# A cross-attention block on one core: reordering the steady loop (query product 7, feature scaling, row loads, query seed)

## The chip, the cores and the metric

The kernel runs on one core of a Trainium2 chip. It is written in a language in which each engine has its own queue and works through it in the order in which the program issues to it; semaphores hold an instruction until what it reads or overwrites is ready. The engines are PE (matrix products; PEld is its loading of weights), DVE (VectorE), ACT (ScalarE), POOL (GpSimd) and SP (SyncE, which here issues nearly all DMAs). The metric is the device time of one execution in microseconds (us), as the median of several runs; lower is better.

## The reference

16 batches of 1024 rows of 512 features attend to 64 context rows each. Rows and context are normalised, scaled and shifted by factors that come from a condition vector; the attention has 16 heads of width 32.

```
xq  = (1 + scale_q[b])  * layernorm(x)       + shift_q[b]
xkv = (1 + scale_kv[b]) * layernorm(context) + shift_kv[b]
q = xq @ Wq + bq;   k, v = split(xkv @ Wkv + bkv)
attn = softmax(q k^T / sqrt(32))             # per batch and head
out = x + (attn v) @ Wp + bp
```

All of it is float32.

## The kernel before

The 16384 rows are worked in 32 blocks of 512 rows (two blocks a batch). Block numbers are `i`; a loop runs over `i = 3 .. 29`, and what comes ahead of it and behind it is written out as straight code. The order of the work is written by hand: no scheduler moves anything, so what stands first in the code stands first in its engine's queue. An iteration works on several blocks at once, in a software pipeline:

- **Block i + 5** is loaded from memory (`load_x`, L119, 1 MB in one DMA). A load for block i + 5 goes into the buffer of block i + 3, of which there are two in turn, and so comes behind `turn(i + 3)`.
- **Block i + 4** has its row statistics taken (`q_stats`, DVE, L294 and L295, two instructions for each of four groups of rows) and their scale computed (`q_scale`, ACT and POOL, L303 to L312).
- **Block i + 3** is normalised (`hidden`, ACT, L335), turned by DVE in 32 x 32 pieces (`turn`, L365, four instructions, into the one buffer `ht`) and moved by 16 DMAs of 64 KB to where rows and features have changed places (`move`, L387, from `ht` to `xt`).
- **Block f = i + 2** has its features scaled and shifted on ACT (`scale_features`, L447, four instructions, in place on `xt`) and sums of its halves formed on POOL (`feature_sums`, L498).
- **Block n = i + 1** has its queries computed. The 512 x 512 matrix product is done in seven half-size products (a Strassen-like scheme): `query_product(n, 1..7)` on PE (L539), eight rows in the trace for each. They go into two PSUM banks. Product 1 starts bank 0; `query_seed` (ACT, L551) copies it into bank 1, where product 2 adds to it; product 7 starts bank 1 anew and product 4 adds to that. In between the finished parts are taken out, by ACT with the bias (`query_out`, L578, two instructions) or by DVE as an addition (`query_added`, L585). So product 4 may not begin before `query_out(n, 7)` has read bank 1, and product 3 not before `query_added(n, 5)` has read bank 0.
- **Block i** has its scores computed (`scores`: PE L670, maxima on DVE L687, copies on ACT L696), the maxima spread (L716) and subtracted on POOL (`subtract`, L729), and the exponentials taken on ACT (`weights(i, 0)` and `weights(i, 1)`, L740). POOL adds the two halves (`total`, L790); DVE sums them (`row_total`, L795) and inverts them, and `inverse_rows` sends the sums through DRAM by one DMA (L813) and four (L815). `swapped` (L745, two DMAs) moves parts of one half into places of the other.
- **Block a = i - 1** has those parts written again by two more exponentials (`again`, ACT, L751), is multiplied with the values (`mix`, PE L860), divided by the row sums (`divided`, DVE L839), and begins its output projection, seven products again: `product(a, 1)`, `product(a, 2)`, `product(a, 7)` (PE L1000), additions to the residual `added` (DVE, L1024), `biased` (ACT, L963: the bias put into a bank that products then add to) and `row_sums` (POOL, L975 to L980). `biased(a, 3)` reuses the bank that `added(a, 2)` reads.
- **Block b = i - 2** ends its projection (products 6, 5, 4, 3) and is stored (L1026).

On SP all DMAs stand in one queue, and a DMA whose data isn't ready holds up those behind it. The program gives them eight semaphores in turn, so each also waits for the eighth DMA ahead of it to land. In an iteration the order on SP is: output stores of b, residual load (L126), rows load (L119), the two swaps (L745), the small store and the four small loads of the row sums (L813, L815), and the 16 moves (L387).

Of the kernel before, what the change touches and what calls it, by code (L numbers as in the profile page):

```python
# [10 lines left out]
AF = mybir.ActivationFunctionType  # L11
# [9 lines left out]
def cross_attention_block(  # L21
# [18 lines left out]
    nc = tc.nc  # L40
# [10 lines left out]
    NB = B * BPB  # L51
# [320 lines left out]
    def features_tile(i):  # L372
        if i in GROUPS:
            pool, tag = (big, "big0") if i == "A" else (qpool, "vb")
            t = pool.tile([P, NC, TB], F32, tag=tag, name=f"xk_{i}", bufs=1)
        else:
            t = qpool.tile([P, 4, NC, NT * 32], F32, tag="xt", name=f"xt_{i}")
        xt_tiles[i] = t
        return t

    def move(i, two=False):

        ht = ht_tiles.pop(i)
        xt = features_tile(i)
        for k in range(4):
            for g in range(4):
                (nc.gpsimd if two and g % 2 else nc.sync).dma_start(  # L387
                    xt[32 * k : 32 * k + 32, g],
                    ht[32 * g : 32 * g + 32, k].rearrange("p c t b -> p c (t b)"),
                )  # L390
# [165 lines left out]
    def query_product(i, n):  # L556
        seven(i, "q", n, (0, 1))

    def query_seed(i):
        seed(i, "q", (0, 1))  # L560
# [183 lines left out]
            at = 64 * g  # L744
            nc.sync.dma_start(s_tiles[i, 1][at : at + 32], s_tiles[i, 0][at + 32 : at + 64])  # L745

    def again(i):
        s = raw_tiles.pop(i)
        for g in range(2):
            at = 64 * g  # L750
            nc.scalar.activation(  # L751
                s_tiles[i, 0][at + 32 : at + 64], s[at : at + 32], AF.Exp, scale=SCALE
            )

    def sums(i, z):
        if z == 0:
# [252 lines left out]
    def added(i, n):  # L1009

        m, o = {1: (0, 0), 2: (0, 0), 6: (0, 1), 7: (1, 1), 5: (1, 1), 4: (0, 1), 3: (1, 0)}[n]
        r = r_tiles[i][:, 2 * m : 2 * m + 2, o * HO : (o + 1) * HO]
        k = acc_bank(i, n)
        a = acc[k].rearrange("p (t h) -> p t h", t=2)
        if i == NB - 1:

            for ts in ((0,), (1,)) if n == 3 else ((0, 1),):
                ts = slice(ts[0], ts[-1] + 1)
                nc.vector.tensor_add(r[:, ts, :], a[:, ts, :], r[:, ts, :])
                if n in (2, 3, 4, 5):  # L1020
                    dst = rows_of(out, i)[:, 2 * m : 2 * m + 2, o * HO : (o + 1) * HO]
                    nc.sync.dma_start(dst[:, ts, :], r[:, ts, :])
            return
        nc.vector.tensor_add(r, a, r)  # L1024
        if n in (3, 4):
            nc.sync.dma_start(  # L1026
                rows_of(out, i)[:, 2 * m : 2 * m + 2, :], r_tiles[i][:, 2 * m : 2 * m + 2, :]
            )
# [421 lines left out]
    for i in range(3, NB - 2):  # L1450
        a, b, n, f = i - 1, i - 2, i + 1, i + 2

        scores(i, 0, crossed=True)
        again(a)
        product(b, 6)
        added(b, 6)
        query_product(n, 1)
        query_seed(n)
        added(b, 7)
        scores(i, 1)  # L1460
        product(b, 5)
        added(b, 5)
        maxima(i)
        subtract(i)
        product(b, 4)
        if i < NB - 3:
            hidden(i + 3, (0, 1, 2))
        query_product(n, 2)
        query_out(n, 2)
        product(b, 3)  # L1470
        spread_rows(a)
        if i < NB - 3:
            hidden(i + 3, (3,))
        added(b, 4)
        added(b, 3)
        biased(a, 2)
        load_residual(i)
        mix(a)
        divided(a)
        row_sums(a, 0)  # L1480
        query_product(n, 6)
        weights(i, 0)
        query_out(n, 6)
        scale_features(f, (0, 1))
        product(a, 1)
        if i + 4 < NB:
            q_stats(i + 4, (0,))
        added(a, 1)
        product(a, 2)
        if i + 4 < NB:  # L1490
            q_stats(i + 4, (1,))
        added(a, 2)
        weights(i, 1)
        total(i)
        query_product(n, 7)
        query_out(n, 7)
        biased(a, 3)
        scale_features(f, (2, 3))
        row_sums(a, 1)
        if i < NB - 3:  # L1500
            turn(i + 3, range(NT))
        if i < NB - 5:
            load_x(i + 5)
        elif i == NB - 3:
            load_residual(NB - 1)
        swapped(i)
        query_product(n, 5)
        query_added(n, 5)
        if i + 4 < NB:
            q_stats(i + 4, (2,))  # L1510
        query_product(n, 4)
        query_added(n, 4)
        if i + 4 < NB:
            q_stats(i + 4, (3,))
        query_product(n, 3)
        query_out(n, 3)
        feature_sums(f)
        product(a, 7)
        row_total(i)
        inverse_rows(i)  # L1520
        if i + 3 < NB:
            move(i + 3)
        if i + 4 < NB:
            q_scale(i + 4)

    y, z = NB - 2, NB - 1
    residual(y - 1)
    scores(y, 0, crossed=True)
    again(y - 1)
    product(y - 2, 6)  # L1530
    added(y - 2, 6)
    query_product(z, 1)
    query_seed(z)
    added(y - 2, 7)
    scores(y, 1)
    product(y - 2, 5)
# [125 lines left out]
```

## Time and profile before

| | |
|---|---|
| median of 3 runs | 1034.76 us (1033.57 to 1035.35) |
| the profiled execution | 1033.38 us, span 1031.6 us |
| granted PE clock, mean over the span | 0.996 |
| PE, DVE, POOL, ACT busy | 97%, 84%, 78%, 72% of the span |
| ahead of the loop's scores(3, 0) | 162.85 us |
| the loop, 27 iterations | 791.56 us (162.85 to 954.41) |
| behind it | 77.19 us (954.41 to 1031.60) |

The span runs from the first to the last instruction of the profiled execution. The timelines list instructions in the order of time: start, length, engine, line, operation, what it writes and reads, shape and count (neighbours of one kind are merged), and in brackets how long the engine stood idle before it and what ended that. Lengths of matmuls overlap, since they are pipelined; how fast PE goes is read from start to start. A wait for several things is put down to the one that the profile saw last, which need not be the true one.

### The profile page before, as it was taken

How to read it: one execution, taken by the hardware profiler on the slowest of the kernel's cores; microseconds unless marked ns; L12 is line 12 of the kernel's file. 1: busy time of each engine (PE TensorE's matmuls, PEld its weight loads, DVE VectorE, ACT ScalarE, POOL GpSimd, SP SyncE). 2: the span in 40 equal slices, each digit the busy share in tenths (PEclk: the TensorE clock that was granted, in tenths of full speed). 3: DMA queues.
4: the chain of work that ended last, by engine and by line, in shares of the span. 5: the costliest groups of instructions: out<-in, count | busy, mean ns of one | idle time of the engine just before them, and what ended most of it. 6: DMA issues, size and time to landing. Idle time of an engine off the chain costs nothing.

```text
span 1031.6 us, 19531 instructions
## 1 busy us (share of the span) xinstructions
PE 1004.2 (97%) x7181; PEld 754.1 (73%) x7181; DVE 862.1 (84%) x1174; ACT 743.0 (72%) x1081; POOL 806.6 (78%) x518
## 2 busy tenths in 40 slices
PE   8999898899999999999999999999999999999998
PEld 7877556677777777777777777777777777777646
DVE  6777668789898888898898988898998988876695
ACT  3777567677887778777887787777877787777630
POOL 4566687788888788988788888988887888888861
PEclk9999999999999999999999999999999999999999
DMA  9574645555455555565455555565455555445222
GB/s 313 166 198 124 151 120 146 174 179 185 135 142 175 150 174 177 174 183 176 135 152 174 150 173 179 172 185 166 143 148 160 165 174 173 139 145 158 72 86 85
DMA packets 114880, 164.41 MB, mean 159 GB/s; under 512 B 35000, under 2 KB 46288, under 8 KB 112992
## 3 DMA queue, kind: packets, MB, share of 16 engines
q1 hardware_dynamic: 114400, 162.62, 52.5%
q8 instruction: 57, 0.93, 0.4%
q0 software_dynamic: 384, 0.54, 0.3%
q14 instruction: 39, 0.32, 0.1%
HBM read 79.21 MB, written 34.60 MB: 110 GB/s over the span
## 4 chain that ended last, share of the span: by engine, by line
PE 62%; SPq 10%; DMA 7%; POOL 6%; DVE 6%; ACT 5%; issue 4%; DVEq 0%; ACTq 0%; POOLq 0%
PE pq L539 25%; PE pp L1000 24%; SPq L387 8%; PE ps L670 5%; PE po L860 3%; POOL s L729 3%; POOL sum L790 2%; DMA xt<-ht 2%; DMA ltd<-lt 2%; ACT xt L447 1%; ACT p L740 1%; PE pp L898 1%; PE pk_A L539 1%; PE pv_A L539 1%; DVE lt L795 1%
## 5 line engine op out<-in xcount | busy, mean ns | idle before, releaser
L729 POOL TENSOR_TENSOR s<-s,mb 128x2048 f32<-128x2048 f32 x64 | 290.6, 4564 | 128.0 <-DVE mb L716 126.2
L687 DVE TRANSPOSE_TENSOR_REDUCE m<-ps 128x32 f32<-128x1024 f32 x128 | 151.1, 1217 | 31.2 <-PE ps L670 31.1
L696 ACT COPY s<-ps 128x1024 f32<-128x1024 f32 x128 | 126.6, 1014 | 62.5 <-PE ps L670 39.0
L1000 PE MATMUL pp<-w_p_sb,ot 128*128 128x256 f32 x720 | 165.7, 380 | 1.0 <-DVE ot L839 0.4
L578 ACT ACTIVATE qt<-pq,bias_t 128x256 f32<-128x256 f32 x256 | 105.4, 462 | 67.3 <-PE pq L539 67.3
L1024 DVE TENSOR_TENSOR r<-pp,r 128x512 f32<-128x512 f32 x203 | 131.8, 670 | 25.3 <-PE pp L1000 19.1
L1000 PEld LDWEIGHTS pp<-w_p_sb,ot 128*128 128x128 f32 x720 | 136.7, 190 | 20.8 <-issue 1.4
L790 POOL TENSOR_TENSOR sum<-s,p 128x2048 f32<-128x2048 f32 x28 | 127.0, 4535 | 4.6 <-ACT p L740 3.8
L1000 PEld LDWEIGHTS pp<-WT,s 128*128 128x128 f32 x480 | 86.6, 190 | 56.9 <-issue 17.6
L539 PE MATMUL pq<-xt_sums,w_q_sums 128*128 128x256 f32 x512 | 123.4, 385 | 0.0
L539 PE MATMUL pq<-xt,w_q_sums 128*128 128x256 f32 x512 | 121.6, 381 | 1.7 <-DVE qt L585 1.7
L539 PE MATMUL pq<-xt,w_q_sb 128*128 128x256 f32 x512 | 121.9, 381 | 1.4 <-ACT pq L551 0.8
L539 PEld LDWEIGHTS pq<-xt_sums,w_q_sums 128*128 128x128 f32 x512 | 95.1, 190 | 36.3 <-issue 24.8
L1000 PE MATMUL pp<-WT,s 128*128 128x256 f32 x480 | 119.4, 392 | 0.2 <-POOL s L979 0.2
L1000 PE MATMUL pp<-WT,ot 128*128 128x256 f32 x480 | 113.6, 380 | 0.5 <-POOL ot L976 0.5
L751 ACT ACTIVATE s<-s 32x2048 f32<-32x2048 f32 x56 | 106.9, 1908 | 5.7 <-DMA p<-s 4.3
L539 PEld LDWEIGHTS pq<-xt,w_q_sb 128*128 128x128 f32 x512 | 96.7, 190 | 17.9 <-ACT pq L551 2.5
L539 PEld LDWEIGHTS pq<-xt,w_q_sums 128*128 128x128 f32 x512 | 97.9, 191 | 15.4 <-DVE qt L585 2.1
L447 ACT ACTIVATE xt<-xt,ss_q 128x512 f32<-128x512 f32 x124 | 94.0, 808 | 16.3 <-DMA xt<-ht 12.2
L1000 PEld LDWEIGHTS pp<-WT,ot 128*128 128x128 f32 x480 | 91.2, 190 | 13.9 <-POOL ot L976 0.9
L335 ACT ACTIVATE x<-x,rstdq 128x512 f32<-128x512 f32 x128 | 97.0, 805 | 5.1 <-POOL rstdq L312 4.4
L498 POOL TENSOR_TENSOR xt_sums<-xt 128x512 f32<-128x512 f32 x64 | 81.5, 1274 | 14.6 <-ACT xt L447 7.8
(187 smaller groups left out, 1632.8 us busy)
## 6 DMA issues: line engine op xcount, KB each, us to landing
x<-in_x_dram SPq DMA_DIRECT2D x32, 1024.0 KB, 7.6
r<-in_x_dram SPq DMA_DIRECT2D x32, 1024.0 KB, 5.5
xt<-ht SPq DMA_DIRECT2D x488, 64.0 KB, 2.0
out_dram<-r SPq DMA_DIRECT2D x58, 512.0 KB, 3.7
p<-s SPq DMA_DIRECT2D x56, 256.0 KB, 4.7
out_dram<-r SPq DMA_DIRECT2D x11, 256.0 KB, 2.2
wss_kv<-in_L_xcond_Wss_kv_dram SPq DMA_DIRECT2D x4, 512.0 KB, 8.0
wss_q<-in_L_xcond_Wss_q_dram SPq DMA_DIRECT2D x4, 512.0 KB, 10.7
```

The costliest lines, as they stand in the source:

```text
L335: nc.scalar.activation(dst, src, AF.Identity, bias=rstd[:, 1, j : j + 1], scale=rstd[:, 0, j : j + 1])
L387: (nc.gpsimd if two and g % 2 else nc.sync).dma_start(xt[32 * k : 32 * k + 32, g], ht[32 * g : 32 * g + 32, k].rearrange("p c t b -> p c ( ...
L447: nc.scalar.activation(xt[:, :, c, :], xt[:, :, c, :], AF.Identity, scale=ss["q"][:, c, b : b + 1], bias=ss["q"][:, NC + c, b : b + 1],)
L539: nc.tensor.matmul(out_, lhsT=lhsT, rhs=rhs, start=new and m == 0 and c == 0, stop=c == HC - 1, skip_group_check=True,)
L578: nc.scalar.activation(dst, src, AF.Identity, bias=bq_t[:, o : o + 1])
L687: nc.vector.tensor_reduce(m_tiles[i][:, z, 2 * e : 2 * e + 2, :], s_banks[i, z][e].rearrange("p r (j a) -> p r j a", a=32), AX.X, ALU.max, ...
L696: nc.scalar.copy(s_tiles[i, z][:, 2 * e : 2 * e + 2, :], s_banks[i, z][e])
L729: eng.tensor_tensor(s_tiles[i, z], s_tiles[i, z], mb_tiles[i], ALU.subtract)
L751: nc.scalar.activation(s_tiles[i, 0][at + 32 : at + 64], s[at : at + 32], AF.Exp, scale=SCALE)
L790: nc.gpsimd.tensor_tensor(t, s_tiles[i, 0], s_tiles[i, 1], ALU.add)
L1000: nc.tensor.matmul(acc[k][:, t * HO : (t + 1) * HO], lhsT=rows[:, c, t * P : (t + 1) * P], rhs=cols[:, c, :], start=n == 2 and t == 0 and ...
L1024: nc.vector.tensor_add(r, a, r)
```

## The change

Four things change place in the loop; no instruction's work changes.

- `query_product(n, 7)` and `query_out(n, 7)` stand ahead of `product(a, 2)` and of `weights(i, 1)`, not behind them.
- `scale_features(f)` is done in one piece, behind `biased(a, 3)`, not two instructions ahead of `weights(i, 1)` and two behind `biased(a, 3)`. `turn(i + 3)` stands ahead of `added(a, 2)`.
- `load_x(i + 5)` leaves its place ahead of `swapped(i)` and goes between the fourth and the fifth of the 16 moves, at the iteration's end.
- `query_seed(n)` stands between the two exponentials of `again`, not behind both. This is also done in block y = 30, behind the loop.

```diff
@@ -378,11 +378,14 @@
         xt_tiles[i] = t
         return t
 
-    def move(i, two=False):
-
-        ht = ht_tiles.pop(i)
-        xt = features_tile(i)
-        for k in range(4):
+    def move(i, two=False, ks=range(4)):
+
+        if ks[0] == 0:
+            features_tile(i)
+        ht, xt = ht_tiles[i], xt_tiles[i]
+        if ks[-1] == 3:
+            ht_tiles.pop(i)
+        for k in ks:
             for g in range(4):
                 (nc.gpsimd if two and g % 2 else nc.sync).dma_start(
                     xt[32 * k : 32 * k + 32, g],
@@ -744,13 +747,13 @@
             at = 64 * g
             nc.sync.dma_start(s_tiles[i, 1][at : at + 32], s_tiles[i, 0][at + 32 : at + 64])
 
-    def again(i):
-        s = raw_tiles.pop(i)
-        for g in range(2):
-            at = 64 * g
-            nc.scalar.activation(
-                s_tiles[i, 0][at + 32 : at + 64], s[at : at + 32], AF.Exp, scale=SCALE
-            )
+    def again(i, g):
+        at = 64 * g
+        nc.scalar.activation(
+            s_tiles[i, 0][at + 32 : at + 64], raw_tiles[i][at : at + 32], AF.Exp, scale=SCALE
+        )
+        if g == 1:
+            raw_tiles.pop(i)
 
     def sums(i, z):
         if z == 0:
@@ -1451,11 +1454,12 @@
         a, b, n, f = i - 1, i - 2, i + 1, i + 2
 
         scores(i, 0, crossed=True)
-        again(a)
+        again(a, 0)
         product(b, 6)
         added(b, 6)
         query_product(n, 1)
         query_seed(n)
+        again(a, 1)
         added(b, 7)
         scores(i, 1)
         product(b, 5)
@@ -1481,27 +1485,24 @@
         query_product(n, 6)
         weights(i, 0)
         query_out(n, 6)
-        scale_features(f, (0, 1))
         product(a, 1)
         if i + 4 < NB:
             q_stats(i + 4, (0,))
         added(a, 1)
-        product(a, 2)
+        query_product(n, 7)
+        query_out(n, 7)
         if i + 4 < NB:
             q_stats(i + 4, (1,))
-        added(a, 2)
         weights(i, 1)
         total(i)
-        query_product(n, 7)
-        query_out(n, 7)
-        biased(a, 3)
-        scale_features(f, (2, 3))
-        row_sums(a, 1)
+        product(a, 2)
         if i < NB - 3:
             turn(i + 3, range(NT))
-        if i < NB - 5:
-            load_x(i + 5)
-        elif i == NB - 3:
+        added(a, 2)
+        biased(a, 3)
+        scale_features(f)
+        row_sums(a, 1)
+        if i == NB - 3:
             load_residual(NB - 1)
         swapped(i)
         query_product(n, 5)
@@ -1519,18 +1520,22 @@
         row_total(i)
         inverse_rows(i)
         if i + 3 < NB:
-            move(i + 3)
+            move(i + 3, ks=(0,))
+            if i < NB - 5:
+                load_x(i + 5)
+            move(i + 3, ks=(1, 2, 3))
         if i + 4 < NB:
             q_scale(i + 4)
 
     y, z = NB - 2, NB - 1
     residual(y - 1)
     scores(y, 0, crossed=True)
-    again(y - 1)
+    again(y - 1, 0)
     product(y - 2, 6)
     added(y - 2, 6)
     query_product(z, 1)
     query_seed(z)
+    again(y - 1, 1)
     added(y - 2, 7)
     scores(y, 1)
     product(y - 2, 5)
```

The order on ACT, from the first exponential of block i = 14 to copy 3 of its neighbour's queries, is before (`s` and `p` are the scores and weights, `qt` the queries, `pq` the banks of their products by number, `xt` the features; "x2" counts neighbours of one kind):

```order
L740 ACTIVATE s_0_4333<-s_0_4333 128x2048
L578 ACTIVATE qt_4398<-pq_1_4345,bias_t 128x2x4x32 x2
L447 ACTIVATE xt_4286<-xt_4286,ss_q 128x4x128 x2
L740 ACTIVATE p_4467<-s_1_4371 128x2048
L578 ACTIVATE qt_4398<-pq_7_4471,bias_t 128x2x4x32 x2
L963 COPY pp_3_4478<-b_diff 128x512
L447 ACTIVATE xt_4286<-xt_4286,ss_q 128x4x128 x2
L578 ACTIVATE qt_4398<-pq_1_4345,bias_t 128x2x4x32 x2
```

and now, with line numbers three higher:

```order
L743 ACTIVATE s_0_4333<-s_0_4333 128x2048
L581 ACTIVATE qt_4398<-pq_1_4344,bias_t 128x2x4x32 x2
L581 ACTIVATE qt_4398<-pq_7_4456,bias_t 128x2x4x32 x2
L743 ACTIVATE p_4466<-s_1_4371 128x2048
L966 COPY pp_3_4481<-b_diff 128x512
L450 ACTIVATE xt_4284<-xt_4284,ss_q 128x4x128 x4
L581 ACTIVATE qt_4398<-pq_1_4344,bias_t 128x2x4x32 x2
```

The copies of product 7 have gone ahead of the second exponential (`p<-s`), and all four scalings stand behind the bias.

On DVE, from the second half of the division to the first addition of the queries, in the same iteration (`r` is the residual that the products are added to, `ht` the turned rows, `bs` and `mvq` the statistics):

```order
L839 TENSOR_TENSOR ot_4434<-po_1_4417,vb_4405 128x1024
L294 BN_STATS bs<-x_4240 128x6
L295 BN_AGGR mvq_4453<-bs 128x2
L1024 TENSOR_TENSOR r_4164<-pp_2_4412,r_4164 128x2x256
L294 BN_STATS bs<-x_4240 128x6
L295 BN_AGGR mvq_4453<-bs 128x2
L1024 TENSOR_TENSOR r_4164<-pp_2_4458,r_4164 128x2x256
L365 STREAM_TRANSPOSE ht_4485<-x_3990 128x4x4x32 x4
L585 TENSOR_TENSOR qt_4398<-pq_1_4345,qt_4398 128x2x4x32 x2
```

and now:

```order
L842 TENSOR_TENSOR ot_4434<-po_1_4417,vb_4405 128x1024
L294 BN_STATS bs<-x_4289 128x6
L295 BN_AGGR mvq_4451<-bs 128x2
L1027 TENSOR_TENSOR r_4164<-pp_2_4412,r_4164 128x2x256
L294 BN_STATS bs<-x_4289 128x6
L295 BN_AGGR mvq_4451<-bs 128x2
L365 STREAM_TRANSPOSE ht_4475<-x_4039 128x4x4x32 x4
L1027 TENSOR_TENSOR r_4164<-pp_2_4470,r_4164 128x2x256
L588 TENSOR_TENSOR qt_4398<-pq_1_4344,qt_4398 128x2x4x32 x2
```

The four transposes have changed places with the addition of product 2.

On SP, from the swaps of one block to those of the next (`ltd` and `vr` are the row sums in DRAM and back, `r` and `x` the residual and the rows):

```order
L745 DMA p_4217<-s_0_4083 32x2048 x2
L813 DMA ltd_4280<-lt_4276 128x64
L815 DMA vr_4279<-ltd_4280 32x4x16 x4
L387 DMA xt_4286<-ht_4235 32x512 x16
L1026 DMA out_dram<-r_3914 128x2x512 x2
L126 DMA r_4414<-in_x_dram 128x4x512
L119 DMA x_4490<-in_x_dram 128x4x512
L745 DMA p_4467<-s_0_4333 32x2048 x2
```

and now:

```order
L748 DMA p_4216<-s_0_4083 32x2048 x2
L816 DMA ltd_4278<-lt_4274 128x64
L818 DMA vr_4277<-ltd_4278 32x4x16 x4
L390 DMA xt_4284<-ht_4225 32x512 x4
L119 DMA x_4289<-in_x_dram 128x4x512
L390 DMA xt_4284<-ht_4225 32x512 x12
L1029 DMA out_dram<-r_3914 128x2x512 x2
L126 DMA r_4414<-in_x_dram 128x4x512
L748 DMA p_4466<-s_0_4333 32x2048 x2
```

The rows' load has left its place behind the residual load and stands behind the fourth move; it is the next iteration's time before it is reached. On PE, where the seven products stand between `mix(a)` and the next scores, `query_product(n, 7)` and `product(a, 2)` have changed places and nothing else.

## The prediction

> **What bounds the kernel now.** I read the busy times on the page first, then one table of stages, then the timelines of a clean and of a late iteration, engine by engine. Below, q1 to q7 are `query_product(n, 1..7)`, p1 to p7 `product(.., 1..7)`, and an iteration starts with the first matmul of `scores(i, 0)`.
>
> ```profile
> PE 1004.2 (97%) x7181; PEld 754.1 (73%) x7181; DVE 862.1 (84%) x1174; ACT 743.0 (72%) x1081; POOL 806.6 (78%) x518
> ```
>
> PE is the bound: all that can be won without taking out matmuls is its idle or slowed time. The stages (start:end, length, busy time of each engine, granted clock after the last count):
>
> ```profile
> 162.85:197.34 34.49, 31.29 (x209) 23.18 (x209) 27.16 (x35) 22.90 (x32) 24.86 (x16) 0.95 0.66 199
> 190.30:193.30 3.00, 3.00 (x9) 2.42 (x10) 1.10 (x3) 1.79 (x3) 3.00 (x1) 0.60 0.89 295
> 547.31:576.21 28.90, 28.90 (x210) 21.95 (x209) 25.86 (x35) 22.90 (x33) 24.40 (x16) 1.00 0.56 166
> 197.34:954.41 757.07, 752.61 (x5409) 570.40 (x5408) 663.91 (x864) 591.23 (x820) 631.96 (x385) 1.00 0.54 162
> ```
>
> The first row is the loop's first iteration (i=3), the third a clean one (i=16), the fourth the other 26. A clean iteration is 28.90; the 26 take 757.07, which is 757.07 - 26 x 28.90 = 5.7 us more, and i=3 takes 5.6 us more. Where PE loses them, the timeline of PE tells (start, length, line, out<-in, count, idle before):
>
> ```profile
> 513.06 1.97 PE L539 MATMUL pq<-xt_sums,w_q_sb 128*128 128x256 f32 x8 [0.78 <-ACT qt L578]
> ...
> 563.91 3.62 PE L1000 MATMUL pp<-w_p_sb,ot 128*128 128x256 f32 x16
> 567.37 1.89 PE L539 MATMUL pq<-xt_sums,w_q_sums 128*128 128x256 f32 x8
> 569.09 1.89 PE L539 MATMUL pq<-xt,w_q_sums 128*128 128x256 f32 x8
> 570.86 1.97 PE L539 MATMUL pq<-xt_sums,w_q_sb 128*128 128x256 f32 x8
> 572.66 1.89 PE L539 MATMUL pq<-xt,w_q_sums 128*128 128x256 f32 x8
> ```
>
> These are p1 and p2 in one row, q7, q5, q4, q3. In the late iteration (i=14) q4 stands idle 0.78 us for ACT: it accumulates into q7's bank, which `query_out(n, 7)` has to read first. In the clean one no idle is printed, yet starts lie 1.77 (q5 to q4) and 1.80 (q4 to q3) apart, where q7 to q5 is 1.72: q4 is held there too, by about 0.12 us. ACT shows why:
>
> ```profile
> 508.87 1.52 ACT L447 ACTIVATE xt<-xt,ss_q 128x512 f32<-128x512 f32 x2 [1.37 <-DMA out_dram<-r]
> 510.30 1.89 ACT L740 ACTIVATE p<-s 128x2048 f32<-128x2048 f32 x1
> 512.10 0.81 ACT L578 ACTIVATE qt<-pq,bias_t 128x256 f32<-128x256 f32 x2
> ...
> 568.08 1.91 ACT L740 ACTIVATE p<-s 128x2048 f32<-128x2048 f32 x1 [0.48 <-POOL s L729]
> 569.89 0.82 ACT L578 ACTIVATE qt<-pq,bias_t 128x256 f32<-128x256 f32 x2
> 570.60 0.60 ACT L963 COPY pp<-b_diff 128x512 f32<-128x512 f32 x1
> 571.12 1.52 ACT L447 ACTIVATE xt<-xt,ss_q 128x512 f32<-128x512 f32 x2
> 574.59 0.84 ACT L578 ACTIVATE qt<-pq,bias_t 128x256 f32<-128x256 f32 x2 [1.95 <-PE pq L539]
> ```
>
> Copy 7 ends at 512.91 late and 570.71 clean, and q4 starts 0.15 behind it both times: the same wait, in its long and its short form. It is long where feature scaling (L447), two places ahead of it, waits 1.37 us. The row names an output store, but what L447 reads is `xt`, so I take the moves of `xt`, on the same DMA queue, as the releaser.
>
> **The change, part by part.**
>
> *Query 7 and its copies ahead of the second exponential, scaling behind it.* PE's work stays the same; q7 and p2 swap, 1.72 us each. q7 ends at 563.91 + 2 x 1.73 = 567.4 instead of 569.1, its copies run 567.6 to 568.4. The second exponential, which could start at 568.08, starts about 568.4 and ends at 570.3. Behind it `total` is queued on POOL, and that was bound by POOL itself:
>
> ```profile
> 570.60 4.55 POOL L790 TENSOR_TENSOR sum<-s,p 128x2048 f32<-128x2048 f32 x1
> ```
>
> It begins at 570.60 either way: cost nothing, with 0.3 us of cover. q4 then finds its bank free more than 2 us ahead. What is gained: the 5.7 us of late iterations, and 26 x 0.12 = 3.1 us. The second is bounded below by nothing, should the spacing belong to that pair of products, and above by 3.1; I take 3.1, because the 0.15 us from copy to q4 is the same in both rows.
>
> *Turning ahead of `added(a, 2)`.* On DVE the four transposes now come first:
>
> ```profile
> 564.57 0.68 DVE L294 BATCH_NORM_STATS2 bs<-x 128x6 f32<-128x512 f32 x1
> ...
> 567.57 0.69 DVE L1024 TENSOR_TENSOR r<-pp,r 128x512 f32<-128x512 f32 x1
> 568.17 2.48 DVE L365 STREAM_TRANSPOSE ht<-x 128x512 f32<-128x512 f32 x4
> 571.09 0.76 DVE L585 TENSOR_TENSOR qt<-pq,qt 128x256 f32<-128x256 f32 x2 [0.43 <-PE pq L539]
> ```
>
> Turn 567.4 to 569.9, addition 2 to 570.5, then `query_added(n, 5)` at its old 571.09. Addition 2 releases `biased(a, 3)`: 570.6 to 571.2. Behind that stand all four scalings, 4 x 0.74 = 3.0 us, to 574.2, and copy 3, which waited until 574.59 for PE anyway. So this too costs nothing, with 0.4 us of cover (0.3 once PE is 0.1 earlier).
>
> But turn waits for one thing more: the moves out of the single `ht` buffer must have landed. If it starts at T, addition 5 ends at T + 2.48 + 0.6 + 0.76 = T + 3.8, and q3, due near 572.5, reads that bank. Less 0.1 for the signal, PE stands from T = 568.6 on, which is 21.3 us into the iteration (start 547.31), and so if the last move lands after about 21.1.
>
> *Row load among the moves.* SP's queue in the clean iteration:
>
> ```profile
> 549.19 0.35 SPq L813 DMA_DIRECT2D ltd<-lt  x1
> 551.09 1.76 SPq L815 DMA_DIRECT2D vr<-ltd  x4
> 552.95 11.01 SPq L387 DMA_DIRECT2D xt<-ht  x16
> ```
>
> The 1 MB load leaves its place in front of `swapped`, so the swap and this small round trip no longer queue behind it; it goes in after move 4. The only such load in the trace that has moves behind it is the one of rows 4, before the loop:
>
> ```profile
> 76.08 0.51 SPq L119 DMA_DIRECT2D x<-in_x_dram  x1
> 76.69 10.96 SPq L387 DMA_DIRECT2D xt<-ht  x16
> ```
> ```profile
> x<-in_x_dram SPq DMA_DIRECT2D x1, 1024.0 KB, 6.0
> ```
> ```profile
> DMA to landing us min/median/max: 5.5/7.7/11.3
> ```
> ```profile
> xt<-ht SPq DMA_DIRECT2D x488, 64.0 KB, 2.0
> ```
>
> It landed after 6.0 us (second fence; the third is the spread of all loads of rows, the last the moves with their median). All loads of rows lie between 5.5 and 11.3, but those of the loop are issued with the residual load in flight, and that won't be so here: I take 6.0. Semaphores go round in eights, so the eighth DMA behind the load waits for it to land. A move takes 10.96 / 16 = 0.69 us of SP at most. From the iteration's start: small store issued 1.9, its landing 1.9 later (3.8), four reads 1.9 (5.6), four moves 2.5 (8.2), load landed 6.0 later (14.2), four more steps of moves 2.6 (16.8), and 2.0 to land: 18.8. That is 2.3 us ahead of the 21.1 from which it hurts. The rows themselves are wanted by the first statistics, at 564.57 on DVE, 17.3 us in; 14.2 is 3 us early. No cost.
>
> *First iteration, i=3.* Here the moves are those issued before the loop, untouched.
>
> ```profile
> 185.64 1.89 PE L539 MATMUL pq<-xt,w_q_sums 128*128 128x256 f32 x8
> 190.30 3.20 PE L539 MATMUL pq<-xt_sums,w_q_sb 128*128 128x256 f32 x8 [2.77 <-ACT qt L578]
> 193.29 2.39 PE L539 MATMUL pq<-xt,w_q_sums 128*128 128x256 f32 x8
> ```
> ```profile
> 186.18 2.49 DVE L365 STREAM_TRANSPOSE ht<-x 128x512 f32<-128x512 f32 x4 [1.37 <-DMA xt<-ht]
> ```
>
> q4 can now start at 187.4 instead of 190.30. But turn still waits until 186.18, and what was behind it is later: addition 2 ends 189.3, addition 5 at 190.0, so q3 starts at 190.1, not 189.1. `biased` ends 189.9, scaling 192.9, copy 3 at 193.7, and the next scores follow at 193.8 instead of 197.34. Gain 3.5 us; of the stall of 2.77, one us stays and moves to q3.
>
> Part of this is clock: behind the 2.8 us gap the granted clock was 0.60 for 3 us, and q4 and q3 took 2.99 and 2.23 us from start to start instead of 1.8 and 1.73, 1.7 us together. The Trainium skill (TensorE: Matmul & The Clock Gate, What's actually happening) lets the clock fall only after an idle window of about 3.4 us; by it these 1.7 us would not hang on this gap, the gain here would be 1.8 and the forecast 1.7 us later. Here a shorter gap was enough, so the row decides.
>
> *Seed between the two repeats.* In the loop q2 comes late enough; only at y=30 does it wait:
>
> ```profile
> 962.79 1.56 PE L539 MATMUL pq<-xt,w_q_sb 128*128 128x256 f32 x6 [0.59 <-ACT pq L551]
> ```
> The seed goes ahead of one of two exponentials; those quoted above, of as many elements in a row, take 1.9 us, three times the stall. So the 0.6 goes; the second repeat ends when it did, and nothing behind it moves.
>
> *Sum:* 5.7 + 3.1 + 3.5 + 0.6 = 12.9 us. For moves that land late now and then I give back 0.5: gain 12.4. The profiled execution took 1033.38 us, of which the span is 1031.6; it would take 1021.0. The median of the runs lies 1.4 above it, so 1034.76 - 12.4 = 1022.4.
>
> **Rivals.** *Slower: the load holds the moves.* SP then waits for the load's landing, the moves land late, turn waits on DVE, and PE at q3 stalls. With a landing of L us the last move lands at 12.8 + L; PE pays from L = 8.3, one us for each us, in the 24 iterations that follow a load. Against it stands the 6.0; for it the median 7.7 and the 11.3. At L = 9.5 it is 24 x 1.2 = 29 us less 12.4: about 1051. From L = 8.8 the gain is gone.
>
> *Half: q4's spacing is its own, or the waits come back elsewhere.* If 1.77 and 1.80 belong to these two products, 3.1 us stay: 1025.5. If besides that the landing varies as it does now, and 8 iterations pay 0.3 us at q3, another 2.4 stay: 1028. For it: the cover on ACT is only 0.3 us.
>
> *No change: the load takes what it mostly takes in the loop today.* At L = 8.8 it gives back what the copies gain: 24 x 0.5 = 12 us, about 1034.
>
> *The clock.* If the slow stretch of i=3 does not hang on the gap, its 1.7 us stay: 1024.1. Against it: the stretch begins with the gap's end, and the row of the other 26 iterations says 1.00.
>
> **How the numbers follow.** The forecast (1020 to 1024) gets 0.62, the clock 0.04, half 0.18 (1024.5 to 1030), no change 0.06, slower 0.10. The range takes in the first three, and below them what it would be without the 0.5 and with runs 2 us lower: 1019.5 to 1029. About 0.2% (2 us) is what a measurement of this kernel can tell from no change. Faster by more 0.84, within 0.06, slower 0.10.
>
> **What would show it.** Right: iterations near 28.78 in the stages; no q4 row with idle time from ACT; i=3 near 31 with a wait of q3 for DVE; the load in the loop landing in 6 to 7 us. Wrong: turn (L365, three lines further down after the change) waiting for `xt<-ht` in most iterations, statistics waiting for `x`, or the second exponential's `total` starting after POOL is free.

## The result, and the profile after

| | before | changed |
|---|---|---|
| median of 4 runs each | 1035.05 us (1033.57 to 1039.84) | 1021.0 us (1020.62 to 1024.54) |
| ratio, 95% interval | | 0.9864 (0.9825 to 0.9903) |
| the profiled execution, its span | 1033.38, 1031.6 us | 1020.62, 1018.8 us |

The changed kernel is faster by 1.0 to 1.8%; 1021.0 was measured where 1022.4 was forecast. One execution of the kernel before, in the second set of the experiments below, took 4545.52 us and is left out of its median and ratios. Busy times on the page of the changed kernel:

```profile
PE 998.9 (98%) x7181; PEld 754.6 (74%) x7181; DVE 859.4 (84%) x1174; ACT 745.2 (73%) x1081; POOL 806.2 (79%) x518
```

PE is busy 5.3 us less with the same 7181 matmuls: time in which it ran slowly or was held within a product counts as busy. The stages of the changed kernel (start:end, length, busy time of each engine, granted clock after the last count): i = 3, a clean iteration (i = 13), the other 26, and what follows the loop.

```profile
161.56:193.01 31.45, 29.64 (x208) 21.96 (x209) 26.06 (x35) 22.33 (x29) 24.65 (x16) 1.00 0.59 174
452.07:480.86 28.79, 28.79 (x209) 21.99 (x209) 25.88 (x35) 23.03 (x33) 24.41 (x16) 1.00 0.56 167
193.01:942.21 749.20, 748.67 (x5409) 571.60 (x5408) 662.62 (x865) 593.79 (x823) 631.87 (x385) 1.00 0.56 165
942.21:1018.84 76.63, 69.97 (x521) 46.63 (x520) 54.25 (x59) 25.48 (x27) 44.13 (x23) 1.00 0.26 86
```

From start to start of the first scores, 25 of the 26 iterations take 28.785 us, and one, i = 22, takes 29.58. 26 x 28.785 = 748.41, so 0.8 us of 749.20 is lost, all of it there; before, 5.7 us were. Where q4 stood, PE now goes on without a break (the timeline of PE, i = 13: q7, p2, q5, q4, q3):

```profile
470.40 1.89 PE L542 MATMUL pq<-xt_sums,w_q_sums 128*128 128x256 f32 x8
472.13 1.89 PE L1003 MATMUL pp<-w_p_sb,ot 128*128 128x256 f32 x8
...
473.86 1.89 PE L542 MATMUL pq<-xt,w_q_sums 128*128 128x256 f32 x8
475.58 1.89 PE L542 MATMUL pq<-xt_sums,w_q_sb 128*128 128x256 f32 x8
477.31 1.89 PE L542 MATMUL pq<-xt,w_q_sums 128*128 128x256 f32 x8
```

q5 to q4 is 1.72 and q4 to q3 1.73, where 1.77 and 1.80 stood: the short form of the wait is gone in every iteration. ACT in the same iteration, and POOL's `total`:

```profile
472.33 0.84 ACT L581 ACTIVATE qt<-pq,bias_t 128x256 f32<-128x256 f32 x2 [1.37 <-PE pq L542]
473.06 1.91 ACT L743 ACTIVATE p<-s 128x2048 f32<-128x2048 f32 x1
475.46 0.59 ACT L966 COPY pp<-b_diff 128x512 f32<-128x512 f32 x1 [0.49 <-DVE r L1027]
475.99 2.93 ACT L450 ACTIVATE xt<-xt,ss_q 128x512 f32<-128x512 f32 x4
479.24 0.84 ACT L581 ACTIVATE qt<-pq,bias_t 128x256 f32<-128x256 f32 x2 [0.32 <-PE pq L542]
```
```profile
475.35 4.55 POOL L793 TENSOR_TENSOR sum<-s,p 128x2048 f32<-128x2048 f32 x1
```

The copies end at 473.17, 2.4 us ahead of q4; the second exponential ends 0.4 us before `total` starts, and the scalings 0.3 us before copy 3, which still waits for PE. The covers of 0.3 to 0.4 us held.

The one late iteration, i = 22, shows what the load's new place can cost. SP from the small store on, then DVE's turn, then q3:

```profile
713.14 0.35 SPq L816 DMA_DIRECT2D ltd<-lt  x1
714.65 1.75 SPq L818 DMA_DIRECT2D vr<-ltd  x4
716.50 2.41 SPq L390 DMA_DIRECT2D xt<-ht  x4
718.96 0.58 SPq L119 DMA_DIRECT2D x<-in_x_dram  x1
719.58 12.04 SPq L390 DMA_DIRECT2D xt<-ht  x12
```
```profile
733.28 2.49 DVE L365 STREAM_TRANSPOSE ht<-x 128x512 f32<-128x512 f32 x4 [2.05 <-DMA xt<-ht]
```
```profile
737.07 1.99 PE L542 MATMUL pq<-xt,w_q_sums 128*128 128x256 f32 x8 [0.53 <-DVE qt L588]
```

By its landing record the load took 9.61 us here (6.05 to 7.58 in the 23 others). The last move landed 21.92 us into the iteration, turn began 0.2 behind it, and the iteration is 0.80 us longer: 21.92 - 0.80 = 21.12, where the prediction put the bound at about 21.1.

In i = 3 what is left of the stall stands at q3, behind a turn that waits for the moves (PE: q4, q3, the next scores; then DVE):

```profile
186.15 1.89 PE L542 MATMUL pq<-xt_sums,w_q_sb 128*128 128x256 f32 x8
189.36 1.99 PE L542 MATMUL pq<-xt,w_q_sums 128*128 128x256 f32 x8 [1.32 <-DVE qt L588]
...
193.01 1.07 PE L673 MATMUL ps<-qt,K_A 32*32 32x512 f32 x22
```
```profile
185.57 2.49 DVE L365 STREAM_TRANSPOSE ht<-x 128x512 f32<-128x512 f32 x4 [2.84 <-DMA xt<-ht]
```

### The profile page after: what moved, and what is told of

It is laid out like the page before. It is cut to its first block, busy times and chain, and to the rows that moved or that the text cites. A ratio compares the mean times of both kernels' runs of the same rounds, so it can differ in the third digit from the quotient of the medians.

```text
span 1018.8 us, 19500 instructions
## 1 busy us (share of the span) xinstructions
PE 998.9 (98%) x7181; PEld 754.6 (74%) x7181; DVE 859.4 (84%) x1174; ACT 745.2 (73%) x1081; POOL 806.2 (79%) x518
## 4 chain that ended last, share of the span: by engine, by line
PE 80%; DMA 5%; SPq 5%; DVE 5%; POOL 2%; ACT 2%; issue 2%; DVEq 0%; POOLq 0%
PE pp L1003 32%; PE pq L542 32%; PE ps L673 6%; PE po L863 4%; SPq L390 3%; DMA xt<-ht 1%; PE pk_A L542 1%; PE pv_A L542 1%; PE pv_B L542 1%; POOL s L732 1%; DMA r<-in_x_dram 1%; DMA x<-in_x_dram 1%; DVE ht L365 1%; DVE m L690 1%; DMA ltd<-lt 1%
## 5 line engine op out<-in xcount | busy, mean ns | idle before, releaser
L1003 PE MATMUL pp<-w_p_sb,ot 128*128 128x256 f32 x720 | 170.0, 379 | 1.0 <-DVE ot L842 0.5
L1003 PEld LDWEIGHTS pp<-w_p_sb,ot 128*128 128x128 f32 x720 | 136.5, 190 | 21.1 <-issue 1.3
L1027 DVE TENSOR_TENSOR r<-pp,r 128x512 f32<-128x512 f32 x203 | 130.9, 666 | 21.9 <-PE pp L1003 18.8
L365 DVE STREAM_TRANSPOSE ht<-x 128x512 f32<-128x512 f32 x124 | 78.3, 682 | 21.8 <-DMA xt<-ht 11.3
```

The lines of the kernel that those rows point to most:

```text
L365: nc.vector.transpose(ht_tiles[i][:, :, :, t, :].rearrange("p k c b -> p c k b"), x_tiles[i][:, t, :].rearrange("p (c k b) -> p c k b", c= ...
L1003: nc.tensor.matmul(acc[k][:, t * HO : (t + 1) * HO], lhsT=rows[:, c, t * P : (t + 1) * P], rhs=cols[:, c, :], start=n == 2 and t == 0 and ...
```

## The experiments

Twelve kernels ran, in three sets of four, each set on a chip of its own. Each kernel was timed beside the kernel before on its chip, which had there medians of 1037.35, 1036.76 and 1037.55 us and scattered more than in the first runs (1031.2 to 1041.8 in the first set, 1032.4 to 1044.0 in the third). In the first two sets account A is the prediction's, in which copies and scaling carry the gain and the load's new place costs and brings little; B holds that the load's place carries part of it. In the third, R holds that the place in SP's queue decides, and the others deny it, each as its words say.

### One part alone

**Seed.** `query_seed` between the two exponentials of `again`, all else as before:

```diff
-        again(a)
+        again(a, 0)
         ...
         query_seed(n)
+        again(a, 1)
```

> Only the seed between the two repeats; the rest as before. Account A (PE waits at query product 4 for the copies of product 7, and the scaling that stands ahead of them makes that wait long): the wait of query product 2 in block y=30 (0.59 us) goes and nothing else changes, clean iterations stay at 28.90, 0.6 us faster than before (profiled about 1032.8). Account B (the gain comes from the row load's new place, which lets the moves land earlier): no change outside y=30 either. This run prices the term, it does not tell A from B.

1034.96 us, ratio 0.9996 (0.9974 to 1.0019). The part from scores(30, 0) to the end took 76.34 us instead of 77.19, and PE no longer stands at q2 there. The whole time can't resolve the 0.6 forecast for it; the stage agrees in size.

**Copies ahead**, with turn, scaling and load where they were:

```diff
         added(a, 1)
+        query_product(n, 7)
+        query_out(n, 7)
         ...
         total(i)
-        query_product(n, 7)
-        query_out(n, 7)
```

> Query product 7 and its copies ahead of product(a,2) and of the second exponential; the turn stays behind the addition of product 2, scaling and load as before. Account A: query product 4 no longer waits, but the addition of product 2 now waits for PE until 22.0 us into the iteration, the four transposes run 22.6 to 25.1 and the addition of query product 5 ends at 25.8, so query product 3, due at 25.1, waits 0.7 to 0.8 us in every iteration: about 29.5 us an iteration, 1036 to 1042 us, no gain at all. Account B: the late iterations stay as they are and clean ones at 28.8 to 28.9, 1030 to 1034.

1042.76 us, ratio 1.0057 (1.0031 to 1.0083): slower alone, as expected. The waits of this kernel (in all, times, longest) show the new one:

```profile
PE pq L539 <- DVE qt L585: 10.5, 26, 1.2
```

q3 waits for addition 5 in 26 iterations, since p2 comes later, addition 2 waits for it, and turn stands behind addition 2. Clean iterations are 29.42 instead of 28.90. So turning ahead of `added(a, 2)` is no ornament: the copies need it.

**Scaling in one piece**, with copies and load where they were:

```diff
         query_out(n, 6)
-        scale_features(f, (0, 1))
         ...
         biased(a, 3)
-        scale_features(f, (2, 3))
+        scale_features(f)
```

> Only the feature scaling in one piece behind the bias; copies of product 7 behind the second exponential, load and turn as before. Account A: the long waits go, the short one at query product 4 (0.12 us) stays: all of iterations 4 to 29 at 28.90 to 28.92, the first one near 31, together 8 to 9.5 us faster than before, about 1024 to 1026. Account B: less than 3 us faster.

1036.93 us, ratio 1.0 (0.9966 to 1.0034): account A, which gave this edit the 5.7 us of the late iterations, missed. Waits of the kernel before, then of this one:

```profile
ACT xt L447 <- DMA xt<-ht: 12.2, 10, 3.8
...
PE pq L539 <- ACT qt L578: 7.2, 8, 2.8
...
ACT s L751 <- DMA p<-s: 4.3, 5, 1.4
```
```profile
ACT s L751 <- DMA p<-s: 31.0, 20, 4.0
...
PE pq L539 <- ACT pq L551: 11.5, 12, 2.4
```

The scaling's waits for the moves are gone, and so are q4's for the copies. In their place the repeats (`again`) wait 31.0 us for the swaps, and q2 waits 12 times for the seed behind them. One such place: SP, ACT and PE around the start of i = 19 at 631.76.

```profile
626.04 0.38 SPq L126 DMA_DIRECT2D r<-in_x_dram  x1
626.52 0.45 SPq L119 DMA_DIRECT2D x<-in_x_dram  x1
630.72 1.16 SPq L745 DMA_DIRECT2D p<-s  x2
```
```profile
638.37 3.84 ACT L751 ACTIVATE s<-s 32x2048 f32<-32x2048 f32 x2 [2.59 <-DMA p<-s]
```
```profile
642.74 1.99 PE L539 MATMUL pq<-xt,w_q_sb 128*128 128x256 f32 x8 [1.47 <-ACT pq L551]
```

The swaps stand behind two loads of 1 MB and land over 7 us after their issue. A delay that DMAs cause had been met at q4; taken away there, it is met at q2.

**Load among the moves**, all else as before:

```diff
-        if i < NB - 5:
-            load_x(i + 5)
         ...
-            move(i + 3)
+            move(i + 3, ks=(0,))
+            if i < NB - 5:
+                load_x(i + 5)
+            move(i + 3, ks=(1, 2, 3))
```

> Only the row load between moves 4 and 5; copies, scaling, turn and seed as before. Account A (scaling waits for the last move and holds up the copies of product 7): the last move lands at 19.4 to 21 us instead of 17.9 to 20.3, the first scaling starts 0.5 to 2 us later than at 18.8, and query product 4 waits for ACT in most of the 24 iterations, 0.3 to 1.5 us each: 10 to 25 us slower than before, 1043 to 1058. Account B (the load's new place is what helps): 5 to 12 us faster.

1045.91 us, ratio 1.009 (1.0056 to 1.0125): slower alone, as A expected. Moves behind the load land later, the two scalings ahead of the second exponential wait for them, and so does q4:

```profile
ACT xt L450 <- DMA xt<-ht: 29.0, 21, 3.6
PE pq L542 <- ACT qt L581: 17.0, 18, 2.8
```

### Parts together

**Copies and turn**, without scaling, load or seed:

```diff
         added(a, 1)
+        query_product(n, 7)
+        query_out(n, 7)
         product(a, 2)
         ...
+        if i < NB - 3:
+            turn(i + 3, range(NT))
         added(a, 2)
         ...
         total(i)
-        query_product(n, 7)
-        query_out(n, 7)
         ...
-        if i < NB - 3:
-            turn(i + 3, range(NT))
```

> As the run with the copies alone, with the turn ahead of the addition of product 2; scaling still half ahead of the copies and the second exponential, load as before. Account A: clean iterations 28.785; where the moves land late (after 18.9 us) the second exponential is late, POOL's addition with it, and part of that comes back at the next scores, 0 to 0.8 us in some 8 iterations; 1020 to 1026 us. Account B: still about 1030, as the moves land no earlier.

1032.56 us, ratio 0.9956 (0.9935 to 0.9977). 17 of the 26 iterations take 28.785, so the 0.12 us each are these two edits' (with the scaling alone clean iterations stayed at 28.90). The others take 28.8 to 30.2, and the time that A gave, 1020 to 1026, was missed.

**All but the load**: the changed kernel with `load_x` back ahead of `swapped`:

```diff
+        if i < NB - 5:
+            load_x(i + 5)
         swapped(i)
         ...
-            move(i + 3, ks=(0,))
-            if i < NB - 5:
-                load_x(i + 5)
-            move(i + 3, ks=(1, 2, 3))
+            move(i + 3)
```

> The changed kernel with the row load back in its old place behind the turn, ahead of the swaps. Account A: the copies no longer hang on the moves, and the moves land by 20.3 us, under the 21.1 at which query product 3 begins to wait: all of iterations 4 to 29 at 28.785, 1019 to 1022, the same as the changed kernel. Account B: most of the gain is lost, 1027 or more.

1033.5 us (1027.38 to 1038.88), ratio 0.9978 (0.9953 to 1.0003): A's 1019 to 1022 was missed, B was right. Without the load's new place nearly all of the gain is gone.

### The load's place

**Behind all 16 moves** instead of behind four:

```diff
-            move(i + 3, ks=(0,))
+            move(i + 3)
             if i < NB - 5:
                 load_x(i + 5)
-            move(i + 3, ks=(1, 2, 3))
```

> The changed kernel with the row load behind all 16 moves. The prediction's bound for the rows (wanted by the statistics 17.3 us into the iteration): the load is issued at about 15.7 and lands at 21.5 to 22.5, DVE stands 4 to 5 us, and as the addition of query product 5 is 1 us ahead of its need, query product 3 waits about 3.2 us in each of 24 iterations: about 75 us slower than the changed kernel, 1085 to 1105, with the granted clock under 1.00 behind the longer gaps. If the rows were not wanted so early: no change.

1114.54 us, ratio 1.0752 (1.0705 to 1.0799), worse still than expected. The statistics wait for the rows, as the prediction's other bound (rows wanted 17.3 us in) says, 26 times:

```profile
DVE bs L294 <- DMA x<-in_x_dram: 113.0, 26, 9.0
```

**The load ahead of the loop too**: the changed kernel with `load_x(7)`, which stood in front of the loop's first small store, put among the moves of block 5.

```diff
-    load_x(7)
     ...
-    move(5)
+    move(5, ks=(0,))
+    load_x(7)
+    move(5, ks=(1, 2, 3))
```

> The changed kernel with the load of rows 7, ahead of the loop, also put between moves 4 and 5 of block 5. If the stall of the first iteration (31.45 us; query product 3 waits 1.3 us for DVE, whose transposes wait for moves that land at 23.7) comes from that load holding up the small store: the moves of that iteration land near 20, the wait goes, the first iteration takes 28.8 to 30, 1.5 to 2.5 us faster than the changed kernel (about 1018.6). If the residual load beside it is what holds the store up: less than 1 us.

1019.49 us (1017.73 to 1020.52), ratio 0.9834 (0.981 to 0.9857): the best median of the study, 1.5 us under the 1021.0 of the changed kernel. That one was not timed beside it, and the two intervals of the ratio overlap, so the whole times don't settle the difference; the stages do. Its windows (i = 3, the other 26):

```profile
163.07:192.37 29.30, 29.30 (x208) 22.03 (x208) 25.68 (x35) 22.40 (x29) 21.99 (x14) 1.00 0.54 161
192.37:940.78 748.41, 748.41 (x5409) 571.61 (x5408) 662.81 (x865) 593.96 (x823) 634.04 (x387) 1.00 0.57 166
```

i = 3 goes from 31.45 to 29.30, so most of the 2.7 us that it had over a clean iteration came from that load, and PE never stands in the 26 iterations behind it.

**Which place it is.** The third set put four kernels on one chip: the changed one, the one with the load back, one with the load back and the residual load among the moves instead, and one with the row load directly behind the swaps.

> The changed kernel once more, beside the next three. Theory R (ring): with the row load behind the residual load, swaps, small store, small loads, moves, output stores and residual load follow one another in one queue, each waiting for the one ahead, and that ring is about as long as an iteration (28.6 us added up from the run with the load back), so a delay in it is hardly made up; with the load among the moves, swaps and store wait for engines and not for the load, and the ring is open. R expects 28.785 in nearly all iterations, 1020 to 1023, and little spread. Theory N (the differences between the runs so far are those of the hour and the chip): spread and time like the run with the load back, 1027 to 1035.

> The changed kernel with the row load back in its old place, once more and beside the changed kernel. R: again slower than the changed kernel, by 5 to 14 us, with iterations in which the repeats on ACT wait for the swaps and the swaps land 5 to 8 us into the iteration. N: the same time as the changed kernel in this call, within 2 us.

```diff
-        load_residual(i)
         mix(a)
         ...
+        if i < NB - 5:
+            load_x(i + 5)
         swapped(i)
         ...
             move(i + 3, ks=(0,))
-            if i < NB - 5:
-                load_x(i + 5)
+        load_residual(i)
+        if i + 3 < NB:
             move(i + 3, ks=(1, 2, 3))
```

> The changed kernel with the two loads exchanged: the row load back in its old place behind the turn, and the residual load in its stead between moves 4 and 5. R: the row load then has no residual load ahead of it, is issued at about 22.9 and lands at 28.5 to 30, so swaps land at about 31 to 32 and the ring is open: 28.785, the same as the changed kernel within 3 us. If it is the row load itself that must not stand ahead of the swaps (theory W), the repeats on ACT wait for the swaps as in the run with the load back, and it is 5 us slower or more.

```diff
         swapped(i)
+        if i < NB - 5:
+            load_x(i + 5)
         ...
-            move(i + 3, ks=(0,))
-            if i < NB - 5:
-                load_x(i + 5)
-            move(i + 3, ks=(1, 2, 3))
+            move(i + 3)
```

> The changed kernel with the row load directly behind the swaps and ahead of the small store. R: swaps are issued at 27.9 and land by 32.5 as in the changed kernel, so the repeats do not wait; the store lands behind the load at about 6 to 7 us, moves begin at 8 to 9 and the last one lands at 19 to 20.5, within the 21.1 that PE bears, and the load's place in the ring is fixed by POOL's addition: nearly all iterations 28.785, within 3 us of the changed kernel. If what counts is the store and the moves behind it (theory M): late transposes, waits of query product 3 or of the projection in many iterations, 5 us slower or more.

| kernel | median, us | range (runs) | ratio to before, 95% |
|---|---|---|---|
| changed | 1023.76 | 1021.58 to 1027.47 (6) | 0.986 (0.9834 to 0.9886) |
| load back | 1034.54 | 1029.59 to 1042.4 (12) | 0.9972 (0.9944 to 0.9999) |
| residual load among the moves | 1025.87 | 1025.09 to 1026.54 (5) | 0.9876 (0.9848 to 0.9904) |
| row load behind the swaps | 1040.35 | 1033.44 to 1043.2 (12) | 1.0012 (0.9992 to 1.0032) |

The first three came out nearly as R expected: the load's place is worth 10.8 us, and moving the other load of the pair does nearly the same. The changed kernel lies 0.8 us above R's 1020 to 1023, and its six runs scatter by 5.9 us. Moving the residual load costs time behind the loop, 81.31 us there against 76.62; its 26 iterations take 748.92 us, those of the changed kernel 749.20 and 749.24 in its two profiles. The fourth R missed: taking the load out from in front of the swaps alone helps nothing. What ends last is read from the traces. Medians of i = 4 to 26 by the DMA records, where these have the landing; us into the iteration that waits for it (the row load: into the one that issues it; the swaps: the second of the two); in the last column the 26 iterations less 26 clean ones (28.785, or 28.90 for the kernel before and the scaling alone):

| kernel | row load lands | swaps land | small store lands | last move lands | lost |
|---|---|---|---|---|---|
| before | 31.7 | 4.1 | 4.7 | 18.7 | 5.7 |
| scaling alone | 33.7 | 5.8 | 6.2 | 20.3 | 12.6 |
| load back (third set) | 34.5 | 7.1 | 7.5 | 21.0 | 13.2 |
| row load behind the swaps | 36.9 | 3.6 | 8.0 | 22.0 | 19.7 |
| residual load among the moves | 28.2 | 3.4 | 3.9 | 19.7 | 0.5 |
| changed (first run) | 15.4 | 3.4 | 3.7 | 19.9 | 0.8 |

SP with the load back, from the small store of i = 13 to the reads of i = 14:

```profile
461.42 0.35 SPq L816 DMA_DIRECT2D ltd<-lt  x1
467.40 1.76 SPq L818 DMA_DIRECT2D vr<-ltd  x4
469.26 10.80 SPq L390 DMA_DIRECT2D xt<-ht  x16
480.15 1.07 SPq L1029 DMA_DIRECT2D out_dram<-r  x2
484.55 0.38 SPq L126 DMA_DIRECT2D r<-in_x_dram  x1
485.03 0.45 SPq L119 DMA_DIRECT2D x<-in_x_dram  x1
488.15 1.15 SPq L748 DMA_DIRECT2D p<-s  x2
491.08 0.35 SPq L816 DMA_DIRECT2D ltd<-lt  x1
496.74 1.76 SPq L818 DMA_DIRECT2D vr<-ltd  x4
```

Every step stands on the one before. The reads wait for the small store, the moves for the reads' place in the queue, the output stores for the moves'; the residual load begins once the stores have landed, the row load half a us behind it, and swaps and small store land behind both. SP's own waits say the same: 153.1 us in 32 places for the small store's landing ahead of the reads (62.2 us in the changed kernel), 99.7 us in 31 for the output stores' ahead of the residual load. From reads to reads it is 496.74 - 467.40 = 29.3 us, more than a clean iteration. This is a ring of DMAs as long as the iteration, so a delay in it stays. Waits of this kernel, then of the one with the load behind the swaps:

```profile
ACT s L752 <- DMA p<-s: 53.7, 24, 3.9
...
DVE ht L365 <- DMA xt<-ht: 27.8, 26, 4.4
```
```profile
DVE ht L365 <- DMA xt<-ht: 48.0, 28, 4.4
...
ACT s L752 <- DMA p<-s: 4.7, 4, 1.9
```

With the load behind the swaps, these are in time, but the small store now waits for the load alone and lands at 8.0. The moves end late, and turn and q3 pay. Add up, over i = 4 to 26, what the last move lands behind 21.1: 20.5 us, where 19.7 were lost; with the load back it is 9.3 of 13.2, the rest being waits at other places. So it isn't enough that the swaps are free of the load: the small store, and with it the moves, has to be. That holds in the two fast kernels: there the last load lands at 28.5 (the residual load of the changed kernel) or 28.2, before the small store is issued at 28.8 + 2.0.

## Why the prediction was right, and where it was not

Terms in us, the profiled execution before against the changed one:

| term | predicted | profile |
|---|---|---|
| late iterations, less late moves | 5.7 - 0.5 | 4.9 (5.7 to 0.8) |
| short form of q4's wait, 26 times | 3.1 | 3.0 (28.90 to 28.785) |
| i = 3 | 3.5 | 3.0 (34.49 to 31.45) |
| seed at y = 30 | 0.6 | 0.6 (77.19 to 76.63) |
| ahead of the loop | 0 | 1.3 (162.85 to 161.56) |
| sum | 12.4 | 12.8 |

**q4's short wait: right, and shown.** It goes wherever copies and turn move (28.785) and stays where they don't (28.90 with the scaling alone). That the spacing was the products' own is ruled out.

**Turn ahead of addition 2: right, and shown** by the copies without it, which cost 0.5 us an iteration. The bound of 21.1 holds at i = 22 (21.12), and sums to the whole loss where the load stands behind the swaps.

**i = 3: the stall right, the clock in part chance, 0.5 too much.** The stall moved to q3, as forecast. Turn waited until 24.0 us into it, not 23.3 as before, because the moves landed later. Granted clock in this stage went from 0.95 to 1.00, with a gap of 1.3 us in it instead of 2.8. That the shorter gap is the reason is not shown. In the seed-only kernel q4 of i = 3 stood as long, and the clock stayed at 1.00 (its q4, then the 3 us from there):

```profile
192.61 1.97 PE L539 MATMUL pq<-xt_sums,w_q_sb 128*128 128x256 f32 x8 [2.74 <-ACT qt L578]
```
```profile
192.60:195.60 3.00, 2.99 (x14) 2.66 (x15) 2.09 (x6) 1.80 (x3) 3.00 (x1) 1.00 0.87 292
```

From q4's start to the next scores it took 5.35 us, where the kernel before took 7.04: the difference is the 1.7 us that the prediction put down to the clock. With the load alone the gap was 2.79 us and the clock behind it 0.50. So of three executions with this stall two paid the clock and one did not, and the prediction, which counted the 1.7 us as sure, was in part lucky that the profiled execution before had paid them. The rival in which the slow stretch does not hang on the gap alone stays open. By the idle window of about 3.4 us that the Trainium skill gives (TensorE: Matmul & The Clock Gate, What's actually happening) the gain here would have been 1.8 by the prediction's working. 3.0 was measured; behind two of the three gaps the clock was lower though they are shorter than that window, and behind the third it was not.

**The 5.7 us: the right size, from the wrong edits.** The step that failed is the one that booked "the 5.7 us of late iterations" under the copies and the scaling, and put the load's new place down as "No cost." and nothing more. The prediction did say that swap and small round trip "no longer queue behind it", and gave that no price. Without it the gain isn't there: 1033.5 and 1034.54 with the load back, 1036.93 for the scaling alone. Copies and scaling took the delay's meeting point away, not the delay, which came in as late DMAs at `again`, at q2 and at turn instead; that is the mechanism of the rival "half", in the case that the load stays. The load alone, on the other hand, is slower, since its moves then hold the scaling that stands ahead of the second exponential. Only together do they leave no delay and nobody waiting at the wrong place. As all were changed at once, the total came out although its terms were booked wrongly; in that it was lucky.

**The load's landing: nearly as taken.** 6.4 us as the median, where 6.0 was taken; it lands at 15.4 and the last move at 19.9, where 14.2 and 18.8 were worked out. The slower rival needed 8.3 and got it once in 24 iterations. It was close: 1.2 us of margin is left to 21.1, and in its second profile the changed kernel has two late iterations, by 0.6 and 0.3 us.

**Ahead of the loop: chance.** The code there is the same, so 1.3 of the 12.8 us are not the change's. Its end lies at 161.56 here, at 163.77 in the third set's profile of the same kernel, and between 162.5 and 164.3 in the other kernels profiled.

Not settled is why the ring's delay is smaller in the kernel before than with the load back. The small store of i = 3 lands 9.7 us into it before and 9.9 with the load back, behind the row load issued ahead of the loop; that of i = 4 lands at 3.6 before, after an i = 3 of 34.49 us, and at 8.6 with the load back, after one of 31.00. A longer i = 3 would let the ring catch up, and a shorter one hand the delay on. That can't be all: the seed-only kernel, with 33.71 us for i = 3 and the small store of i = 4 landing at 5.5, lost 9.5 us, and the first profile of the load back, with 31.64 and 7.0, lost 6.2. Part of the difference may lie in the executions: the profiled one of the kernel before took 1033.38 us, where its medians in the three sets were 1036.8 to 1037.6, and that first profile of the load back took 1027.39, where the median of its ten runs was 1033.5. The kernel that tells it, the load back in the loop and the first load moved, wasn't tried.

## What to carry to other kernels

When a wait is removed, ask where the late transfer behind it is met next: the scaling's wait went away, and the same delay came back at q2, for no gain at all. Draw the DMA queue as a ring over one iteration and add up its length; where it comes near the iteration's (29.3 against 28.8 us here), a big load ahead of a small round trip is on the path, though no engine's row names it. An edit that is slower alone (1.0057, 1.009) may be half of one that is faster (0.9864), so test undoing each part of the whole as well as each part by itself.

## What the runs showed of the hardware

Small DMAs behind a 1 MB load on SP's queue land with it: in i = 22 the load landed at 17.43 and the seven moves behind it at 17.61 to 18.61, the first of them 9.2 us after its issue began, where the moves of this kernel take 2.2 in the median. The Trainium skill (DMA: Bandwidth & Descriptors, Queues, rings and completion order) says that each engine takes the descriptors of one ring in their order; the trace agrees.

A second load half a us behind another pays for both. Row loads on the pages with the load back and with the residual load among the moves (count, size, median us to landing):

```profile
x<-in_x_dram SPq DMA_DIRECT2D x32, 1024.0 KB, 9.1
```
```profile
x<-in_x_dram SPq DMA_DIRECT2D x32, 1024.0 KB, 5.4
```

The scatter of the runs in the third set was wider where the ring is closed: 12.8 us between the fastest and slowest of 12 with the load back and 9.8 of 12 with the load behind the swaps, 5.9 us in the six of the changed kernel and 1.5 in the five with the residual load among the moves. The numbers of runs differ, and the kernel before scatters by 11.5 us in 23, so this is a hint and no more.
